# A GRU on one core: the first two steps of x turned by the matrix array, input weights of one gate in four loads, and the state's columns in another order

## The chip, the core and the metric

The kernel runs on one core of one Trainium2 chip. The metric is the device time of one execution in microseconds (us); the value to beat is the median of three runs. One core has five engines with their own instruction queues: TensorE (PE, the matrix array, with its weight loads listed as PEld), VectorE (DVE), ScalarE (ACT), GpSimd (POOL) and SyncE (SP), which issues most of the DMAs. PE writes to PSUM; weights, x and the state lie in SBUF.

## What is computed

A GRU runs over 128 steps on a batch of 64 with 512 inputs and 512 hidden units, and its states are added to its input:

```python
def step(h, inp):
    x_t, prop = inp
    comb = concatenate([x_t, h], axis=-1)
    z = sigmoid(comb @ Wz + bz)
    r = sigmoid(comb @ Wr + br)
    comb2 = concatenate([x_t, r * h], axis=-1)
    h_cand = tanh(comb2 @ Wh + bh)
    h_new = (1.0 - z) * h + z * h_cand
    h_next = where(prop, tanh(h_new @ Wp + bp), h_new)   # prop: every fourth step but the last
    return h_next, h_new
out = x + all h_new
```

All is float32. Each of Wz, Wr and Wh has 512 rows for x (the input weights) and 512 for the state (the state weights).

## The kernel before

The batch is cut into two halves h of 32 rows. A state tile (`h`, `rh`, `c`, `keep`) has 128 partitions, 32 rows of the batch times four quarters q of the columns, and for each half 128 columns. To be multiplied, a state has to be turned: DVE turns blocks of 32 by 32 (`turn`, line 250), which leaves in partition q * 32 + e and block k what was column q * 128 + k * 32 + e. PE then multiplies, for each k of K = 4, a 128 x 32 block of the turned state with rows of the weights that are laid out to fit (`gate`, line 231).

The recurrence, one generator for each half (`half`, line 836), does in every step: PE r's four products; ACT the sigmoid (`crossed`, line 246, two instructions of 64 partitions) into PSUM (`scratch_r`); DVE the product with the state and the turn (`rhT`); PE z's products, ACT its sigmoids into PSUM (`rec_z`); PE the candidate's products on `rhT`, ACT its tanh into SBUF (`c`); DVE a product, a difference and the turn (`hT`), on which the next step's r begins. On every fourth step the state goes through Wp, a tanh (`hprop`) and a turn. The two halves alternate. `seed` (line 395) puts x's share of the gates and the bias into PSUM ahead of the state's products.

The input products of later steps fill the time in which PE would wait for the state. They are put into a list (`put`, `fill`, lines 410 and 416) from which each half takes so many units at the places that a table gives (`PLACES`, `HEAD`, `TAIL`, lines 623 to 630). So the order of PE's work is fixed when the kernel is built. For steps from 4 on they are done with fewer products (sums of weights, prepared by DVE and POOL: `sum_inner`, `sum_outer`; sums of x by POOL: `four`; sums of results: `batch`, `outer_...`).

Before the recurrence stands a prologue. x of steps 0 to 3 is loaded in quarters of the columns (`load_step`, line 110, four DMAs a step) and turned by DVE (`join_x`, line 258). The input weights (`load_wx`, line 116) come r first, in two pieces, then z and the candidate in one piece each, all on SP's queue. `idle(48)` (line 643) gives PE products of zeros meanwhile. Then come r's input products of steps 0 and 1, z's, the bias spread over the partitions by PE (`spread`, line 190), the candidate's, and with `put` and `both(9)` (lines 681 and 682) step 2's. DVE prepares weight sums between and ends with `sum_outer_1` into `d`, on which POOL starts its own sums. The state weights (`load_w`, line 96) are loaded in four pieces of 32 partitions each, on the queues of SP and ACT, at places between the prologue's products; `later_loads` (line 159: x of steps 4 on, Wp, its bias) stand at the prologue's end. POOL issues the loads of the biases (line 130) and of the first state (line 144), and its first full tensor operation is line 659.

POOL adds h to x for the output (line 811), except in the last step, where DVE does (lines 883 and 915).

Of the kernel before, what the change touches and what calls it, by code (L numbers as in the profile page):

```python
# [9 lines left out]
F32 = mybir.dt.float32  # L10
# [8 lines left out]
def kernel(  # L19
# [14 lines left out]
    nc = tc.nc  # L34
    B, T, D = x.shape
    H = h0.shape[1]
    P = 128
# [29 lines left out]
    nc.vector.memset(zeros, 0.0)  # L67
    ones = const.tile([1, V], F32, name="ones")
    nc.gpsimd.memset(ones, 1.0)
# [16 lines left out]
    def part(q):  # L86
        return slice(q * V, (q + 1) * V)

    def load_x(tile_, t0, n, j=0, engs=(nc.sync, nc.sync)):
        for h in range(S):  # L90
            for q in (0, 2, 1, 3):
                engs[q // 2].dma_start(
                    out=tile_[part(q), j : j + n, h, :], in_=x[ts(h, V), t0 : t0 + n, ts(q, J)]
                )

    def load_w(wt, w, k0=0, k1=K, engs=(nc.sync, nc.sync)):
        for q in (0, 2, 1, 3):
            engs[q // 2].dma_start(
                out=wt[part(q), k0:k1, :],
                in_=w[q * P + k0 * V : q * P + k1 * V, :].rearrange("(k e) n -> e k n", e=V),  # L100
            )

    both_queues = (nc.sync, nc.scalar)
# [3 lines left out]
    def new_xr(g):  # L107
        xr[g] = xrp.tile([P, Q4, S, J], F32, tag="xr", name=f"xr_{g}")

    def load_step(t, engs=both_queues):  # L110
        for q in (0, 2, 1, 3):
            engs[q // 2].dma_start(
                out=xr[0][part(q), t], in_=x[:, t, ts(q, J)].rearrange("(h b) u -> b h u", h=S)
            )

    def load_wx(i, k0, k1):
# [2 lines left out]
            in_=gates_in[i][:D].rearrange("(p k) n -> p k n", k=K)[:, k0:k1],  # L119
        )  # L120

    h_init = two.tile([P, S, J], F32, tag="h", name="h_init")
# [12 lines left out]

    for i in (Z, H_):
        load_wx(i, 0, K)

    for t in (2, 3):
        load_step(t, (nc.sync, nc.sync))  # L140
    held = const.tile([1, 1], F32, name="held")
    nc.gpsimd.tensor_copy(held, wx[0:1, 2, R, 0:1])
    for h in range(S):
        nc.gpsimd.dma_start(
            out=h_init[:, h, :],
            in_=h0[ts(h, V), :].rearrange("b (q j) -> q b j", q=NQ),
        )

    def load_wh(i):
        load_w(wh[i], gates_in[i][D:], engs=both_queues)  # L150

    xs = {}

# [34 lines left out]
        return v.rearrange("p n (d c j) -> p c n d j", d=2, c=2)  # L188

    def spread(bank, rows, which):  # L190
        bank = bank.rearrange("p (i d j) -> p i d j", i=2, d=2)
        for h in range(S):
            for c in range(2):
                nc.tensor.matmul(  # L194
                    bank[part(2 * h + c), 0 : len(which)],
                    lhsT=ones,
                    rhs=quarters(bias_row[:, rows])[:, c],
                    start=True,
                    stop=True,
                )  # L200
        for j, i in enumerate(which):
            nc.scalar.copy(
                bias_x[:, :, :, i, :].rearrange("p n d u -> p d n u"),
                bank[:, j].rearrange("p d (n u) -> p d n u", n=C),
            )
# [30 lines left out]
    def product(ps, h, lT, w, k, start=False):  # L236
# [6 lines left out]
            start,  # L243
        )

    def crossed(dst, h, i, func):
        for d in range(2):
            nc.scalar.activation(dst[ts(d, 2 * V)], gate_ps(i, h)[ts(h, 2 * V), d, :], func)  # L248

    def turn(dst, src):  # L250
        nc.vector.transpose(out=dst, in_=src)
# [6 lines left out]
    def join_x(g, i):  # L258
        if g * Q4 >= T:
            return  # L260
        if g not in xT:
            xT[g] = xtp.tile([P, Q4, C, P], F32, tag="xT", name=f"xT_{g}")
        src = xr[g] if g < FIRST else xs[g]
        nc.vector.transpose(
            out=xT[g][:, i].rearrange("p c (a h b) -> p h (c a) b", a=S, h=S),
            in_=src[:, i].rearrange("p h (e k) -> p h k e", k=K),
        )

    def outer(kb, nb, ka):
        return wx[:, kb * S + ka, :, :].rearrange("p g (q n u) -> p n q g u", q=NQ, n=C)[:, nb]  # L270
# [157 lines left out]

    def banks(t):
        first, second = scratch[:2] if t % 2 == 0 else scratch[2:4]  # L430
        rooms = (first[:, : S * J], first[:, S * J :], second[:, : S * J])
        return (rooms[0], rooms[2], rooms[1]) if t == T - 1 else rooms

# [9 lines left out]
    def plain_unit(t, e, k, start, end=None, gates=()):  # L443
        g, i = divmod(t, Q4)
        bank = (q_bank, q_bank, r_bank) if t % 2 == 0 else (a_bank, a_bank, x_banks[0])
        if t == T - 1:
            bank = (a_bank, x_banks[0], a_bank)
        second = H_ if t == T - 1 else Z
# [200 lines left out]
    for i in (1, 2):  # L649
        sum_inner(i, nc.vector, slice(0, 2))  # L650
    spread(scratch[3], slice(0, 2), (R, H_))
    load_wh(R)
    now(first[Z][1])
    for t in range(2):
        add_bias(t, (R,))
    for h in range(S):
        seed(R, 0, h)
    spread(scratch[4], slice(2, 3), (Z,))
    nc.gpsimd.tensor_sub(bias_d, bias_x[:, 1], bias0)
    load_wh(Z)  # L660
    for t in range(2):
        add_bias(t, (Z,))
    seed(Z, 0, 0)
    load_wh(H_)
    join_x(0, 2)
# [5 lines left out]
    now(sum(first[H_], []))  # L671
    for t in range(2):
        add_bias(t, (H_,))
    join_x(0, 3)
# [2 lines left out]
    for i in (3, 5):  # L677
        sum_inner(i, nc.gpsimd)
    sum_outer(3)
    later_loads()  # L680
    put(plain(2, (R, Z)) + plain(3) + plain(2, (H_,)))
    both(9)

# [73 lines left out]
    def behind_step(t, duo, u, h_new):  # L757
# [50 lines left out]
            if u == 7:  # L808
                sum_s12(even + 2)
        if t < T - 1:  # L810
            nc.gpsimd.tensor_add(xr[g][:, j], xr[g][:, j], h_new)  # L811

        n = 0
        if t >= T - CHUNK:
# [21 lines left out]
    def half(h):  # L836

        for t in range(T):
# [31 lines left out]
            def gate_z(part, halves, h_old=h_old, z_=z_, keep=keep):  # L870
                for i in halves:
                    crossed(z_[:, i, :], i, Z, AF.Sigmoid)
                nc.vector.scalar_tensor_tensor(  # L873
                    out=keep[:, part, :],
                    in0=z_[:, part, :],
                    scalar=1.0,
                    in1=h_old[:, part, :],
                    op0=ALU.subtract,
                    op1=ALU.mult,
                )  # L880
                if last:
                    o = xr[g][:, j, part, :]
                    nc.vector.tensor_sub(o, o, keep[:, part, :])

            if h == 1:
                if late(t):
# [25 lines left out]
            nc.vector.tensor_mul(c, cand[:, h, :], c)  # L912
            if last:
                o = xr[g][:, j, h, :]
                nc.vector.tensor_add(o, c, o)
# [87 lines left out]
```

## Time and profile before

| what | us |
|---|---|
| median of three runs (1259.17 to 1260.79) | 1260.61 |
| the profiled execution's own time | 1259.52 |
| its span, first to last instruction | 1257.6 |
| PE busy | 1250.6 |
| POOL busy | 891.5 |
| ACT busy | 837.9 |
| DVE busy | 805.5 |

In the rows that follow, a time in front is the start in us from the span's start, the number behind it the duration; "x16" is a count of instructions merged into a row; brackets hold the idle time of the engine ahead of it and what ended it. A float32 product counts as two records. A group's row gives its busy time in us and the mean duration of one in ns, then the engine's idle time ahead of the group. In the table by stage, each row gives a stretch, its length, then the busy time and count of PE, PEld, DVE, ACT and POOL, PE's granted clock as a share, the share of DMA engines at work, and GB/s.

### The profile page before, as it was taken

The page shows a single profiled execution, that of the slowest core. Times are in us where ns is not written, and L with a number is a line of the kernel's source. Part 1 is how long each engine was busy: PE and PEld are TensorE (multiplying, and loading weights), DVE is VectorE, ACT ScalarE, POOL GpSimd, SP SyncE. Part 2 cuts the span into 40 slices and gives each one's busy share as a digit, 9 for nine tenths or more (in the row PEclk, how much of TensorE's full clock was granted, in tenths as well). Part 3 has the DMA queues.
Part 4 walks back from the last instruction along what each step waited for, and adds up shares of the span by engine and source line. Part 5 has one row for each costly group of instructions (what it writes and reads, how often), then busy time and mean ns, then how long its engine had stood idle before and what let it go on. Part 6 is the DMA issues. An engine that isn't in the chain of part 4 may idle for free.

```text
span 1257.6 us, 60730 instructions
## 1 busy us (share of the span) xinstructions
PE 1250.6 (99%) x25960; PEld 1162.1 (92%) x25960; DVE 805.5 (64%) x2173; ACT 837.9 (67%) x2685; POOL 891.5 (71%) x1031
## 2 busy tenths in 40 slices
PE   9999999999999999999999999999999999999998
PEld 4899999999999999999999999999999999999975
DVE  4666666666666666666666666666666666666545
ACT  2566666767666666766666667667676666676665
POOL 3988877776876778767788676786777777677530
PEclk9999999999999999999999999999999999999999
DMA  8311112121121110211211111111111111111010
GB/s 240 91 28 45 49 41 53 36 54 39 34 53 48 41 47 26 53 53 37 53 29 43 53 43 47 38 47 41 53 37 49 40 37 53 42 48 37 9 42 23
DMA packets 113232, 60.82 MB, mean 48 GB/s; under 512 B 12836, under 2 KB 109348, under 8 KB 112964
## 3 DMA queue, kind: packets, MB, share of 16 engines
q1 hardware_dynamic: 111268, 55.00, 16.4%
q8 instruction: 205, 3.36, 1.1%
q10 hardware_dynamic: 1440, 1.80, 0.6%
q14 instruction: 63, 0.52, 0.1%
q0 software_dynamic: 256, 0.14, 0.1%
HBM read 40.11 MB, written 16.78 MB: 45 GB/s over the span
## 4 chain that ended last, share of the span: by engine, by line
PE 98%; DMA 1%; issue 1%; DVE 0%; SPq 0%; POOLq 0%; POOL 0%; ACT 0%; ACTq 0%
PE rec L222 44%; PE rec_z L222 16%; PE scratch_r L222 14%; PE scratch_q L222 11%; PE scratch_a L222 5%; PE scratch_x L222 4%; PE scratch_y L222 4%; DMA wx<-in_L_cond_Wr_dram 0%; SPq L821 0%; DMA xr<-in_x_dram 0%; DMA out_dram<-xr 0%; PE scratch_x L194 0%; DVE z L912 0%; POOLq L998 0%; POOL xr L811 0%
## 5 line engine op out<-in xcount | busy, mean ns | idle before, releaser
L222 PE MATMUL rec<-wh,rhT 128*32 128x256 f32 x4096 | 376.3, 379 | 0.0
L222 PE MATMUL rec<-wh,hT 128*32 128x256 f32 x3072 | 282.6, 379 | 0.0
L222 PE MATMUL rec_z<-wh,hT 128*32 128x256 f32 x3072 | 282.5, 379 | 0.0
L222 PEld LDWEIGHTS rec<-wh,rhT 128*32 128x32 f32 x4096 | 249.6, 110 | 21.1 <-ACT rec L398 1.2
L248 ACT ACTIVATE scratch_r<-rec 64x128 f32<-64x128 f32 x512 | 128.2, 250 | 138.3 <-PE rec L222 63.7
L398 ACT COPY rec<-cp 64x256 f32<-64x256 f32 x512 | 190.6, 372 | 19.9 <-DVE cp L437 0.4
L222 PEld LDWEIGHTS rec<-wh,hT 128*32 128x32 f32 x3072 | 187.4, 110 | 14.7 <-issue 1.8
L222 PEld LDWEIGHTS rec_z<-wh,hT 128*32 128x32 f32 x3072 | 193.8, 110 | 7.2
L248 ACT ACTIVATE rec_z<-rec_z 64x128 f32<-64x128 f32 x488 | 122.2, 250 | 90.1 <-PE rec_z L222 78.6
L248 ACT ACTIVATE c<-rec 64x128 f32<-64x128 f32 x512 | 139.7, 273 | 60.4 <-PE rec L222 48.8
L811 POOL TENSOR_TENSOR xr<-xr,h 128x256 f32<-128x256 f32 x127 | 93.2, 734 | 91.6 <-DVE h L925 91.6
L575 POOL TENSOR_TENSOR mb<-mb,mb 128x768 f32<-128x768 f32 x58 | 106.3, 1833 | 66.8 <-DVE mb L541 66.8
L575 POOL TENSOR_TENSOR cp<-mb,mb 128x768 f32<-128x768 f32 x76 | 139.2, 1831 | 9.5 <-DVE mb L541 5.8
L575 POOL TENSOR_TENSOR cp<-mb 128x768 f32<-128x768 f32 x46 | 84.2, 1831 | 57.0 <-ACT rec_z L398 55.5
L222 PE MATMUL scratch_r<-tw,s 128*32 128x192 f32 x928 | 120.9, 326 | 0.0
L514 ACT COPY cq<-scratch_q 128x384 f32<-128x384 f32 x212 | 102.1, 482 | 19.3 <-PE scratch_q L222 17.8
L531 DVE TENSOR_TENSOR cx<-scratch_r,cx 128x384 f32<-128x384 f32 x106 | 59.1, 558 | 84.1 <-PE scratch_r L222 66.8
L222 PE MATMUL scratch_q<-tt,s 128*32 128x192 f32 x928 | 103.7, 326 | 0.0
L873 DVE SCALAR_TENSOR_TENSOR keep<-rec_z,h 128x256 f32<-128x256 f32 x91 | 38.7, 425 | 95.6 <-ACT rec_z L248 94.6
L537 DVE TENSOR_TENSOR mb<-scratch_q,cx 128x384 f32<-128x384 f32 x106 | 59.1, 558 | 62.4 <-ACT cq L514 62.4
L853 DVE TENSOR_TENSOR rh<-scratch_r,h 128x128 f32<-128x128 f32 x192 | 56.1, 292 | 61.2 <-ACT scratch_r L248 61.2
L222 PE MATMUL rec<-wp,hT 128*32 128x256 f32 x992 | 91.5, 379 | 0.1
(188 smaller groups left out, 3846.5 us busy)
## 6 DMA issues: line engine op xcount, KB each, us to landing
out_dram<-xr SPq DMA_DIRECT2D x249, 64.0 KB, 1.8
xr<-in_x_dram SPq DMA_DIRECT2D x248, 64.0 KB, 2.1
xs<-in_x_dram SPq DMA_DIRECT2D x240, 64.0 KB, 2.0
wx<-in_L_cond_Wr_dram SPq DMA_DIRECT2D x2, 512.0 KB, 5.1
wx<-in_L_cond_Wz_dram SPq DMA_DIRECT2D x1, 1024.0 KB, 5.9
wx<-in_L_cond_Wh_dram SPq DMA_DIRECT2D x1, 1024.0 KB, 8.2
wp<-in_L_cond_Wp_dram SPq DMA_DIRECT2D x4, 256.0 KB, 5.3
wh<-in_L_cond_Wr_dram ACTq DMA_DIRECT2D x2, 256.0 KB, 3.8
```

The costliest lines, as they stand in the source:

```text
L222: nc.tensor.matmul(ps[part(2 * h + c)], lhsT=left, rhs=rhs(c), start=start, stop=True, skip_group_check=True,)
L248: nc.scalar.activation(dst[ts(d, 2 * V)], gate_ps(i, h)[ts(h, 2 * V), d, :], func)
L398: nc.scalar.copy(gate_ps(i, h)[rows].rearrange("p d (c n) -> p d c n", c=C), G[t][rows, :, :, i, :].rearrange("p c d n -> p d c n"),)
L514: nc.scalar.copy(c[:, :nm], ps[:, :nm])
L531: nc.vector.tensor_add(T2[what][:, :nm], r_ps[:, :nm], T2[what][:, :nm])
L537: nc.vector.tensor_add(blocks(1, 1), runs(q_ps[:, :nm]), runs(T2[what][:, :nm]))
L575: nc.gpsimd.tensor_add(dst, a, b)
L811: nc.gpsimd.tensor_add(xr[g][:, j], xr[g][:, j], h_new)
L853: nc.vector.tensor_mul(rh[:, h, :], r_, h_old[:, h, :])
L873: nc.vector.scalar_tensor_tensor(out=keep[:, part, :], in0=z_[:, part, :], scalar=1.0, in1=h_old[:, part, :], op0=ALU.subtract, op1=ALU.mult,)
```

## The change

x of steps 0 and 1 is loaded as plain rows (64 batch rows, all 512 columns), one DMA on SP and one on ACT; PE turns it with an identity (`turn_rows`: four transposes a step into PSUM) and DVE copies the result. The identity is made on POOL. x of these steps is loaded again later in the old form, for the output. r's input weights come in four loads, one for each k, and r's products of steps 0 and 1 alternate k by k; z's and the candidate's come in two loads each. The idle products are 24, 8 and 4, around the turns.

State weights are loaded in two pieces over 128 partitions, partition p holding rows 4p to 4p + 3. For that the state's columns have to lie in another order: `crossed` writes its result with `state_order`, 32 groups of four elements with a step of 32 elements, and ACT copies the first state in that order. x and the output keep the plain order, so POOL's sum and the last step's operations on DVE read the state with the step. All loads but one are issued on SP, the later ones in one run behind r's input products.

The diff, cut:

```diff
+    ident = const.tile([B, B], F32, name="ident")
+    make_identity(nc, ident)
...
-    def load_w(wt, w, k0=0, k1=K, engs=(nc.sync, nc.sync)):
-        for q in (0, 2, 1, 3):
-            engs[q // 2].dma_start(
-                out=wt[part(q), k0:k1, :],
-                in_=w[q * P + k0 * V : q * P + k1 * V, :].rearrange("(k e) n -> e k n", e=V),
+    def load_w(wt, w):
+        for k0 in (0, 2):
+            nc.sync.dma_start(
+                out=wt[:, k0 : k0 + 2, :],
+                in_=w.rearrange("(p k) n -> p k n", k=K)[:, k0 : k0 + 2],
             )
...
-    load_step(0)
-    load_wx(R, 0, 2)
-    load_step(1, (nc.scalar, nc.scalar))
+    for t in range(2):
+        both_queues[t].dma_start(out=x_rows[:, ts(t, D)], in_=x[:, t, :])
+    for k in range(K):
+        load_wx(R, k, k + 1)
     for i, b in enumerate((br, bh, bz)):
         nc.gpsimd.dma_start(out=bias_row[:, i, :], in_=b.rearrange("(o n) -> o n", o=1))
-    load_wx(R, 2, K)
...
-    for i in (Z, H_):
-        load_wx(i, 0, K)
-    for t in (2, 3):
-        load_step(t, (nc.sync, nc.sync))
+    for k in (0, 2):
+        load_wx(Z, k, k + 2)
+    load_step(2)
+    for k in (0, 2):
+        load_wx(H_, k, k + 2)
...
+    def plain_order(v):
+        return v.rearrange("p (e k) -> p e k", k=K)
+    def state_order(v):
+        return v.rearrange("p (k e) -> p e k", k=K)
     def crossed(dst, h, i, func):
         for d in range(2):
-            nc.scalar.activation(dst[ts(d, 2 * V)], gate_ps(i, h)[ts(h, 2 * V), d, :], func)
+            nc.scalar.activation(
+                state_order(dst[ts(d, 2 * V)]),
+                plain_order(gate_ps(i, h)[ts(h, 2 * V), d, :]),
+                func,
+            )
...
+    def turn_rows(t, bank):
+        for k in range(K):
+            nc.tensor.transpose(
+                bank[:, ts(k, B)],
+                x_rows[:, ts(t, D)].rearrange("b (p k) -> b k p", k=K)[:, k],
+                ident,
+            )
+        nc.vector.tensor_copy(xT[0][:, t].rearrange("p c n -> p (c n)"), bank[:, : K * B])
...
-    idle(48)
-    join_x(0, 0)
-    now(first[R][0])
-    join_x(0, 1)
-    now(first[R][1])
-    now(first[Z][0])
+    idle(24)
+    turn_rows(0, scratch[4])
+    idle(8)
+    turn_rows(1, scratch[3])
+    idle(4)
+    for k in range(K):
+        for t in range(2):
+            now([first[R][t][k]])
+    spread(scratch[4], slice(0, 2), (R, H_))
     load_wh(R)
+    load_step(3)
+    load_wh(Z)
+    load_wh(H_)
+    load_x(xr[0], 0, 2)
+    later_loads()
+    for half_k in (slice(0, 2), slice(2, K)):
+        for t in range(2):
+            now(first[Z][t][half_k])
...
     for h in range(S):
+        nc.scalar.copy(state_order(h_init[:, h, :]), plain_order(h_rows[:, h, :]))
         turn(hT[:, h, :], h_init[:, h, :])
...
-            nc.gpsimd.tensor_add(xr[g][:, j], xr[g][:, j], h_new)
+            o = xr[g][:, j].rearrange("p h (e k) -> p h e k", k=K)
+            nc.gpsimd.tensor_add(o, o, h_new.rearrange("p h (k e) -> p h e k", k=K))
```

More of the change, by code (lines that the diff above doesn't have):

```diff
@@ L144 @@
         nc.gpsimd.dma_start(
-            out=h_init[:, h, :],
+            out=h_rows[:, h, :],
             in_=h0[ts(h, V), :].rearrange("b (q j) -> q b j", q=NQ),
@@ L149, in load_wh @@
     def load_wh(i):
-        load_w(wh[i], gates_in[i][D:], engs=both_queues)
+        load_w(wh[i], gates_in[i][D:])
     xs = {}
@@ L190, in spread @@
     def spread(bank, rows, which):
-        bank = bank.rearrange("p (i d j) -> p i d j", i=2, d=2)
+        bank = bank.rearrange("p (i d j) -> p i d j", i=len(which), d=2)
         for h in range(S):
@@ L267, in join_x @@
         )
+    def turn_rows(t, bank):
+        if 0 not in xT:
+            xT[0] = xtp.tile([P, Q4, C, P], F32, tag="xT", name="xT_0")
+        for k in range(K):
[3 more added lines that the diff above has]
+                ident,
+            )
+        nc.vector.tensor_copy(xT[0][:, t].rearrange("p c n -> p (c n)"), bank[:, : K * B])
     def outer(kb, nb, ka):
@@ L430, in banks @@
         first, second = scratch[:2] if t % 2 == 0 else scratch[2:4]
+        if t < 2:
+            return first[:, : S * J], second[:, : S * J], scratch[4][:, ts(t, S * J)]
         rooms = (first[:, : S * J], first[:, S * J :], second[:, : S * J])
@@ L447, in plain_unit @@
             bank = (a_bank, x_banks[0], a_bank)
-        second = H_ if t == T - 1 else Z
+        second = H_ if t in (1, T - 1) else None if t == 0 else Z
         return (
@@ L670 @@
         sum_inner(i, nc.vector, slice(2, 3))
-    now(sum(first[H_], []))
+    for half_k in (slice(0, 2), slice(2, K)):
+        for t in range(2):
+            now(first[H_][t][half_k])
     for t in range(2):
@@ L881, in gate_z @@
                 if last:
-                    o = xr[g][:, j, part, :]
-                    nc.vector.tensor_sub(o, o, keep[:, part, :])
+                    o = plain_order(xr[g][:, j, part, :])
+                    nc.vector.tensor_sub(o, o, state_order(keep[:, part, :]))
             if h == 1:
```

28 lines of the change are left out of this document (13 added, 15 removed).

## The prediction

> **What bounds the kernel now.** I read the head of the page, then the table by stage, then the chain that ended last.
>
> ```profile
> span 1257.6 us, 60730 instructions
> PE 1250.6 (99%) x25960; PEld 1162.1 (92%) x25960; DVE 805.5 (64%) x2173; ACT 837.9 (67%) x2685; POOL 891.5 (71%) x1031
> PE 98%; DMA 1%; issue 1%; DVE 0%; SPq 0%; POOLq 0%; POOL 0%; ACT 0%; ACTq 0%
> ```
> ```profile
> 11.12:23.74 12.62, 12.62 (x219) 6.58 (x212) 10.28 (x28) 2.14 (x6) 1.11 (x2) 1.00 0.97 236
> 23.74:60.00 36.26, 36.26 (x751) 28.25 (x750) 20.66 (x55) 18.50 (x59) 35.09 (x36) 1.00 0.48 123
> 60.00:1200.00 1140.00, 1140.00 (x23978) 1086.24 (x23971) 743.89 (x1994) 779.46 (x2496) 840.22 (x974) 1.00 0.16 43
> 1253.00:1257.60 4.60, 0.00 (x0) 0.00 (x0) 0.79 (x3) 0.19 (x1) 0.00 (x0) 0.76 0.11 29
> ```
>
> PE is the bound: from 11.12 to 1200 us it is never idle, its granted clock (the 1.00) is full, and the chain lies on it for 98%. So there are two ways to move the end: the moment at which PE has the first gates behind it, and holes torn into a stream that has none. The chain at the start gives the first:
>
> ```profile
> 0.76 1.70 DMA xr<-in_x_dram
> 2.47 5.59 DMA wx<-in_L_cond_Wr_dram
> 8.06 0.04 issue
> 8.11 1.07 PE scratch_q L222 x16
> 9.19 1.93 PE scratch_a L222 x32
> 11.12 1.73 PE scratch_q L222 x32
> ...
> 23.31 0.43 PE scratch_a L222 x8
> 23.74 1.75 PE rec L222 x28
> ```
>
> PE waits for r's input weights until 8.06, has r of steps 0 and 1 done at 11.12, then works 12.6 us without a gap on z, the candidate and step 2, and enters the recurrence at 23.74.
>
> **The change part by part: the start.** Three things must now be there before r's first product: x as rows, the four slices of r's weights, and the identity. The data come early enough: by the chain the first of x landed at 2.47 us, behind an issue at 0.76.
>
> ```profile
> 6.50:8.00 1.50, 1.03 (x16) 0.43 (x16) 0.00 (x0) 0.00 (x0) 0.00 (x0) 1.00 1.07 370
> ```
>
> At 370 GB/s, 0.25 MB of rows and 1 MB of r take 3.5 us from about 2.5, so they are in by 6 to 7. All that follows on SP in one queue (z, step 2, candidate, step 3, nine state and input pieces, together 6.8 MB up to the last state weight) takes 18 us by the same rate, hence is in at about 21; the recurrence needs it from 27 on. The eight loads of x for steps 0 and 1 and step 4's x follow that and are late for nothing. The new queue costs nothing unless the rate falls below 6.8 MB in 24 us, 280 GB/s.
>
> The identity is another matter. It is made on POOL by a memset and a select. In the order of the kernel before, POOL has one instruction that loads engine code, right in front of its first full tensor operation (L659); in the changed order that load stands in front of the select, second thing on POOL.
>
> ```profile
> 0.75 0.12 POOL L69 MEMSET ones<- 1x32 f32 x1 [0.29 <-POOLq L989]
> ...
> 8.23 1.40 POOL L144 DMA_DIRECT2D h_init<-in_cond_dram  x2
> 16.79 1.01 POOL L659 TENSOR_TENSOR bias_d<-bias_x 128x384 f32<-128x384 f32 x1 [7.15 <-ACT bias_x L202]
> ```
>
> Before, the load sits in a gap of 7.15 us in which POOL waited for bias_x in any case, so it costs between 0 and 7.15. The gap is the only row that holds it; I take most of it, 6.5. [...]
>
> So: memset of ones and identity to 1.0, load to 7.5, select 0.3 (as the 0.12 memset and a little), identity at 7.8, seen by PE at 7.9. PE meanwhile runs out:
>
> ```profile
> 1.20 1.04 PE L212 MATMUL rec<-zeros 128*32 128x512 bf16 x8 [1.20 <-DVE zeros L67]
> 2.03 0.64 PE L212 MATMUL rec_z<-zeros 128*32 128x512 bf16 x4
> 2.46 1.07 PE L212 MATMUL rec<-zeros 128*32 128x512 bf16 x8
> ```
>
> Twelve idle products per 1.26 us are 0.105 each: 24 end at 3.8. PE then stands for 4 us. From 7.9: eight turns in two groups, 0.4 a group (two records at 54 ns each, from 1.73 us for 32 of four times the columns, and the first result's latency), 0.8; twelve idle products 1.3, which hide DVE's two copies out of PSUM (0.42 each, as L873 below). r begins at 10.0. Its work is 2 x 1.73 = 3.5. The last row of the stage table shows the clock at 0.76 in 4.6 us without matmuls, so the hole may also cost clock: between 0 and 3.5 (half speed for all of r); I take 1.4, half speed until about 5 us after the restart. r ends at 14.9 instead of 11.12: **+3.8**. That the four slices are used as they come is worth nothing then: all have landed by 10.0.
>
> Behind r PE has the same 12.6 us. DVE, in order too, starts on r's bias at 14.9 + 1.0 (the bias products) + 0.4 (ScalarE's copy) = 16.3; from there to the turn of step 3's x it has no more than the 10.28 us that it had in the stage from 11.12, so this ends by 26.6. PE wants it at 14.9 + 23.31 - 11.12 = 27.1. No further loss; POOL's weight sums, which follow DVE, start as much later as PE does. The biases of r and the candidate are issued on POOL behind the select; the last of the three took longest before:
>
> ```profile
> tw<-in_L_cond_bz_dram POOLq DMA_DIRECT2D x1, 2.0 KB, 5.4
> ```
>
> From 8 to 9.5 plus 5.4 they are in by 13.4 to 14.9, and r's end is 14.9: just covered; uncovered they would cost what they are late.
>
> **State's columns in another order.** Every activation of the recurrence now writes 32 groups of 4 with a step of 32 elements (128 bytes). No row of before shows ScalarE doing so. Its rows:
>
> ```profile
> L248 ACT ACTIVATE c<-rec 64x128 f32<-64x128 f32 x32 | 8.7, 273 | 3.6 <-PE rec L222 2.9
> L248 ACT ACTIVATE scratch_r<-rec 64x128 f32<-64x128 f32 x32 | 8.0, 250 | 8.0 <-PE rec L222 3.7 <-DVE mb L540 3.4
> L811 POOL TENSOR_TENSOR xr<-xr,h 128x256 f32<-128x256 f32 x8 | 5.9, 737 | 4.2 <-DVE h L925 4.2
> L251 DVE STREAM_TRANSPOSE hT<-h 128x128 f32<-128x128 f32 x16 | 5.0, 312 | 0.5
> L264 DVE STREAM_TRANSPOSE xT<-xs 128x256 f32<-128x256 f32 x8 | 4.9, 635 | 0.1
> ```
> ```profile
> L873 DVE SCALAR_TENSOR_TENSOR keep<-rec_z,h 128x256 f32<-128x256 f32 x91 | 38.7, 425 | 95.6 <-ACT rec_z L248 94.6
> L853 DVE TENSOR_TENSOR rh<-scratch_r,h 128x128 f32<-128x128 f32 x192 | 56.1, 292 | 61.2 <-ACT scratch_r L248 61.2
> ACT rec_z L398 <- POOL cp L575: 0.4, 1, 0.4
> ```
>
> (The first five are groups of the eight steps from 600 to 677 us; the last is the one wait for POOL's sums that the list of waits has.) The nearest is L264, DVE reading SBUF with a step of 16 bytes. 128 more columns cost DVE 0.13 (292 ns against 425), so a plain turn of 256 would be 312 + 130 = 442; it takes 635, 0.19 more for 256 elements. For 128 elements that is 0.10 an instruction, a pair 0.19 to 0.2. [...] I take 0.10 where the target is SBUF as in that row (the tanh's c and hprop) and 0 where it is PSUM (the sigmoids of r and z), for which there is no row.
>
> What 0.19 on the tanh does depends on the margin in front of PE:
>
> ```profile
> 600.13 0.55 ACT L248 ACTIVATE c<-rec 64x128 f32<-64x128 f32 x2 [0.68 <-PE rec L222]
> ...
> 601.37 0.31 DVE L251 STREAM_TRANSPOSE hT<-h 128x128 f32<-128x128 f32 x1
> 601.80 0.14 PEld L222 LDWEIGHTS rec<-wh,hT 128*32 128x32 f32 x2
> ...
> 629.96 0.31 DVE L251 STREAM_TRANSPOSE hT<-h 128x128 f32<-128x128 f32 x1
> 630.79 0.14 PEld L222 LDWEIGHTS rec<-wh,hT 128*32 128x32 f32 x2
> ```
>
> c's tanh, two DVE operations, the turn, PE's weight load stand in one line. From the turn's end to the load it is 0.12 in the first pair and 0.52 in the second; hardly one of the 574 turns has less than 0.12, so that is the signal's own time and the first pair has no reserve. The eight turns of first halves from 601.37 to 668.59 have 0.00, 0.13, 0.12, 0.40, 0.41, 0.38, 0.05 and 0.46 of reserve. Against 0.19 the missing parts are 0.19, 0.06, 0.07 and 0.14: 0.46 us in 76.9. The order of PE's work is fixed, so a hole is never made good. Over 1140 us that is 6.8; second halves, whose tanh queues behind the first's on ScalarE, half as much again: **+10**.
>
> POOL's sum of x and h now reads h with that step: at most again 0.74, likelier 0.2 to 0.4 of it. Over 127 times that is 25 to 94 us of the 366 that POOL is idle. What hides it is that hardly anything waits for POOL: 0.4 us in the whole run. At the end four DVE operations of 128 columns read with the step: **+0.3**, 0.1 each, three on the way out.
>
> **The rivals.** *Strides free, identity late.* The start's 3.8 and at most 0.3 remain: 1264 to 1265 us. For it: L264 is a read, and no row shows a write that suffers; against it: L264 is all there is on this step. *PSUM pays as well.* Then z's four sigmoids (+0.4) stand in front of the tanh on ScalarE, which has only 3.6 / 32 = 0.11 us of idle time ahead of each c, and the turn of r*h has the same 0.12 in its tightest step. The tanh chain is late by some 0.4, so the eight reserves miss 0.4, 0.27, 0.28, 0, 0, 0.02, 0.35 and 0, with 0.4 for r's chain 1.7 a cycle, 25 us, and a quarter more for second halves: +31, 1296 us. [...] *The other side: not slower.* If the code load takes under 2 us, as it may if what it loads is there already, the identity is in time. Then 3.8 + 0.8 + 1.3 gives r's start at 5.9 and its end at 9.4, 1.7 us earlier; DVE's chain, then behind PE by 9.4 + 1.4 + 10.28 = 21.1 against 9.4 + 12.2 = 21.6, gives back at most 0.5 where its waits add up. With free strides the time is 1259 to 1259.5. It decides below about 3 us of load; above 5 it can't. *The change doesn't do what it says:* only in the first forecast's sense, that slices used as they come are used when all are there.
>
> **How the numbers follow.** The profiled execution took 1259.5 us (span 1257.6 and 1.9 around it), 1.1 under the median 1260.6. Sum: 1259.5 + 3.8 + 10 + 0.3 = 1273.6, with the 1.1 back 1274.7. Chances: this case 0.37 (own range 1269 to 1283); strides free 0.27; PSUM too 0.22; not slower 0.10; more than that, as from a step that costs the whole 0.27, 0.04. The range 1262 to 1298 leaves out the not-slower case and the last. 0.2% (2.5 us) is about what a measurement of this kernel can tell from no change: faster 0.06, same 0.09 (the not-slower case and a start with little clock loss), slower 0.85.
>
> **What would show it.** Right: PE idle from about 3.8 to 7.9 with the turns behind POOL's select, the select starting some 6 us after its memset; r done near 15 us; c's rows near 370 ns with scratch_r and rec_z still at 250; weight loads that wait for DVE in the tight steps, and PE's busy share falling under 99% between 60 and 1200 us. Wrong: a select before 4 us; c at 273; r's and z's rows at 350, which is the third case; a state weight that lands after 27 us.

## The result, and the profile after

The changed kernel takes 1280.1 us in the median of 5 runs (1277.98 to 1280.64), against 1260.61 before; the ratio is 1.0151, with a 95% interval of 1.0136 to 1.0166. The prediction was 1274.7, in a range of 1262 to 1298. The profiled execution took 1280.1 with a span of 1278.3, 20.7 more than the span before.

The head of the page and the share of the chain:

```profile
span 1278.3 us, 60724 instructions
PE 1268.0 (99%) x25956; PEld 1150.0 (90%) x25956; DVE 811.8 (64%) x2173; ACT 922.5 (72%) x2687; POOL 910.4 (71%) x1033
PE 97%; ACT 1%; DVE 0%; issue 0%; DMA 0%; ACTq 0%; DVEq 0%
```

PE is still "busy" for 99%, and the table by stage (stretch, length, busy us of PE, weight loads, DVE, ACT, POOL, clock, DMA) shows no hole in the middle either (in the last row PE is idle for 8.8 us, against 5.2 in the last 73.2 us before, which hold the same work of VectorE):

```profile
12.03:24.65 12.62, 12.62 (x218) 6.76 (x220) 10.43 (x29) 2.71 (x8) 1.15 (x1) 1.00 1.00 340
60.00:1200.00 1140.00, 1140.00 (x23697) 1060.62 (x23691) 742.80 (x1970) 844.67 (x2467) 855.22 (x973) 1.00 0.16 42
1200.00:1278.30 78.30, 69.50 (x1230) 49.81 (x1219) 36.97 (x119) 54.10 (x153) 15.91 (x13) 0.99 0.12 29
```

The busy share misleads here. The ends of matmuls are modelled, so a hole of 0.2 us disappears under the modelled length of the one before it. What does not disappear is the count: 23,697 records in the same 1140 us, where there were 23,978, 1.2% fewer; the busy time of the weight loads fell too, from 1086.2 to 1060.6. The honest measure is how late a given piece of work is. The turn of r*h happens once per step and half in every kernel here; its end, taken from the trace and set against the kernel before, says where the time goes:

| end of first half's turn of r*h at | before, us | after, us | late by | added in this part |
|---|---|---|---|---|
| step 0 | 26.76 | 27.67 | 0.91 | 0.91 |
| step 8 | 117.12 | 119.08 | 1.97 | 1.06 |
| step 117 | 1162.68 | 1177.62 | 14.94 | 12.97 |
| step 127 (the last) | 1249.07 | 1268.40 | 19.33 | 4.39 |
| end of the span | 1257.64 | 1278.33 | 20.68 | 1.35 |

**The start.** POOL's first instructions (start, us, engine, line):

```profile
0.75 0.12 POOL L69 MEMSET ones<- 1x32 f32 x1 [0.29 <-POOLq L1027]
0.81 0.14 POOL masks.py:197 MEMSET ident<- 64x64 f32 x1
1.03 0.23 POOL masks.py:199 TENSOR_SCALAR_AFFINE_SELECT ident<-ident 64x64 f32<-64x64 f32 x1
```

The select stands 0.22 us behind its memset, and the identity is there at 1.26 us. The record that the prediction read as the load of engine code did move in front of the select. In the views of the two lines (duration in ns: least, median, most; first and last start in us), before and after:

```profile
L659 POOLq MODIFY_POOL_CONFIG  x2: 37/37/37, 9.6 to 9.7; - x2
```
```profile
masks.py:199 POOLq MODIFY_POOL_CONFIG  x2: 1/1/1, 0.9 to 0.9; - x2
```

But no 6.5 us go by behind it: the select follows within about 0.1. What PE waited for instead is in the chain:

```profile
0.76 3.34 DMA x_rows<-in_x_dram
4.10 0.14 issue
4.24 0.71 PE scratch_y L288 x4
...
7.14 0.85 PE scratch_q L227 x6
7.99 0.85 PE scratch_a L227 x6
8.85 0.85 PE scratch_q L227 x6
9.70 0.60 PE scratch_a L227 x6
10.30 0.43 PE scratch_q L227 x6
...
24.65 1.75 PE rec L227 x28
```

x as rows lands at 4.10, and the same piece of r's product takes 0.85 us until 9.7 and 0.43 from 10.3 on: PE runs at half rate until about 10 us. The table by stage counts 36 records in 3.5 us and then 48 in 2.5, while its clock reads 1.00 in both:

```profile
6.00:9.50 3.50, 3.50 (x36) 1.73 (x40) 0.43 (x1) 0.00 (x0) 1.52 (x3) 1.00 0.91 306
9.50:12.00 2.50, 2.50 (x48) 1.16 (x42) 0.00 (x0) 0.00 (x0) 0.00 (x0) 1.00 1.06 328
```

r ends at 12.03, against 11.12, and the recurrence starts 0.91 us later.

**The state's order.** ScalarE's rows over the whole run (count, busy us, mean ns of one, idle before):

```profile
L259 ACT ACTIVATE c<-rec 64x128 f32<-64x128 f32 x512 | 206.5, 403 | 48.7 <-PE rec L227 39.9
L259 ACT ACTIVATE scratch_r<-rec 64x128 f32<-64x128 f32 x512 | 128.0, 250 | 121.7 <-DVE mb L568 68.1 <-DVE cx L559 24.2 <-PE rec L227 13.8
L259 ACT ACTIVATE rec_z<-rec_z 64x128 f32<-64x128 f32 x488 | 122.0, 250 | 81.7 <-PE rec_z L227 70.1
L259 ACT ACTIVATE hprop<-rec 64x128 f32<-64x128 f32 x124 | 50.1, 404 | 8.8 <-PE rec L227 7.2
L259 ACT ACTIVATE z<-rec_z 64x128 f32<-64x128 f32 x24 | 9.5, 395 | 2.5 <-PE rec_z L227 2.1
```

Each instruction that writes SBUF went from 273 to about 400 ns, tanh and sigmoid alike (z is a sigmoid into SBUF in the late steps); the sigmoids that write PSUM have the same 250 ns as before. So it is the target, not the function, that has the price. The turn of h and PE's load, at the same two turns that the prediction showed:

```profile
609.04 0.31 DVE L266 STREAM_TRANSPOSE hT<-h 128x128 f32<-128x128 f32 x1
609.47 0.14 PEld L227 LDWEIGHTS rec<-wh,hT 128*32 128x32 f32 x3 [0.21 <-issue]
...
638.22 0.31 DVE L266 STREAM_TRANSPOSE hT<-h 128x128 f32<-128x128 f32 x1
638.84 0.14 PEld L227 LDWEIGHTS rec<-wh,hT 128*32 128x32 f32 x2
```

At the first the distance is still 0.12, the signal's own time, only PE's weight loads now wait for it ("0.21 <-issue"); at the second it fell from 0.52 to 0.31. Of the eight first-half turns of a cycle five now stand at 0.12. In the view of the tile hT this is a sum: how long the weight loads sat idle before one that reads hT (us, times). Before:

```profile
  issue: 2.3, 8
  ACT z L248: 0.5, 1
  ACT rec_z L398: 0.5, 1
  ACT rec L928: 0.2, 1
```

and after:

```profile
  issue: 8.4, 36
  ACT rec_z L424: 7.2, 33
  ACT z L259: 2.0, 3
  ACT rec L966: 1.7, 2
```

3.5 us became 19.3. The names are not the cause (ACT's copy had long been done where a load waits for a turn); the tile is.

### The profile page after: what moved, and what is told of

It is laid out like the page before. It is cut to its first block, busy times and chain, and to the rows that moved or that the text cites. A ratio compares the mean times of both kernels' runs of the same rounds, so it can differ in the third digit from the quotient of the medians.

```text
span 1278.3 us, 60724 instructions
## 1 busy us (share of the span) xinstructions
PE 1268.0 (99%) x25956; PEld 1150.0 (90%) x25956; DVE 811.8 (64%) x2173; ACT 922.5 (72%) x2687; POOL 910.4 (71%) x1033
## 3 DMA queue, kind: packets, MB, share of 16 engines
q1 hardware_dynamic: 111604, 56.90, 16.4%
## 4 chain that ended last, share of the span: by engine, by line
PE 97%; ACT 1%; DVE 0%; issue 0%; DMA 0%; ACTq 0%; DVEq 0%
PE rec L227 44%; PE rec_z L227 17%; PE scratch_r L227 11%; PE scratch_q L227 10%; PE scratch_a L227 5%; PE scratch_y L227 5%; PE scratch_x L227 5%; ACT c L259 1%; ACT z L259 0%; DMA x_rows<-in_x_dram 0%; DVE h L963 0%; DVE hT L266 0%; ACT rec L424 0%; PE rec L217 0%; DVE z L950 0%
## 5 line engine op out<-in xcount | busy, mean ns | idle before, releaser
L227 PE MATMUL rec<-wh,rhT 128*32 128x256 f32 x4096 | 393.5, 379 | 0.0
L227 PE MATMUL rec<-wh,hT 128*32 128x256 f32 x3072 | 300.4, 380 | 1.6 <-DVE hT L266 1.1
L227 PE MATMUL rec_z<-wh,hT 128*32 128x256 f32 x3072 | 299.7, 379 | 0.0
L227 PEld LDWEIGHTS rec<-wh,rhT 128*32 128x32 f32 x4096 | 254.0, 110 | 19.3 <-ACT scratch_r L259 2.0
L259 ACT ACTIVATE c<-rec 64x128 f32<-64x128 f32 x512 | 206.5, 403 | 48.7 <-PE rec L227 39.9
L227 PEld LDWEIGHTS rec_z<-wh,hT 128*32 128x32 f32 x3072 | 199.8, 110 | 7.4
L849 POOL TENSOR_TENSOR xr<-xr,h 128x256 f32<-128x256 f32 x127 | 111.2, 876 | 99.0 <-DVE h L963 99.0
L950 DVE TENSOR_TENSOR rec_z<-c,rec_z 128x128 f32<-128x128 f32 x244 | 72.3, 296 | 63.2 <-ACT c L259 63.0
L227 PE MATMUL rec<-wp,hT 128*32 128x256 f32 x992 | 97.0, 379 | 0.8 <-DVE hT L266 0.5
L227 PE MATMUL rec<-wh,hpT 128*32 128x256 f32 x992 | 94.3, 379 | 0.0
L227 PE MATMUL rec_z<-wh,hpT 128*32 128x256 f32 x992 | 94.3, 379 | 0.0
```

The costliest lines, as they stand in the source:

```text
L227: nc.tensor.matmul(ps[part(2 * h + c)], lhsT=left, rhs=rhs(c), start=start, stop=True, skip_group_check=True,)
L259: nc.scalar.activation(state_order(dst[ts(d, 2 * V)]), plain_order(gate_ps(i, h)[ts(h, 2 * V), d, :]), func,)
L849: nc.gpsimd.tensor_add(o, o, h_new.rearrange("p h (k e) -> p h e k", k=K))
```

## The experiments

The theory, W: the stepped write to SBUF costs 0.13 us per tanh on the path from gate to turn and makes nearly all of the loss; the start costs 0.9. Its rivals: R, ScalarE pays for a step on either side; P, GpSimd's slower add or the new loads are the cause; S, the new start shifts the two halves against each other for good. Four runs tell them apart. In the table, "late by" is again the turn of r*h (or the end) against the profile of the kernel before; the ratio is that of the times, on the same chip.

| kernel | median us | ratio, 95% | late at step 0 | 8 | 117 | 127 | end |
|---|---|---|---|---|---|---|---|
| after | 1280.10 | 1.0151 (1.0136 to 1.0166) | 0.91 | 1.97 | 14.94 | 19.33 | 20.68 |
| e1_read_side | 1261.12 | 1.0007 (0.9999 to 1.0016) | 1.40 | 1.86 | 1.67 | 1.40 | 2.11 |
| e2_order_off | 1260.76 | 1.0007 (0.9998 to 1.0016) | -0.76 | 0.00 | -0.19 | -0.47 | 0.23 |
| e3_order_alone | 1279.29 | 1.0154 (1.0138 to 1.0169) | 0.45 | 1.48 | 14.49 | 19.03 | 19.88 |
| e4_tanh_only | 1277.21 | 1.0138 (1.0124 to 1.0152) | -0.87 | 1.82 | 14.63 | 16.97 | 17.84 |
| e5_idle32 | 1260.55 | 1.0006 (0.9997 to 1.0015) | 0.59 | 1.99 | 1.85 | 1.60 | 2.36 |
| e6_add_plain | 1260.97 | 1.0007 (0.9999 to 1.0016) | 0.19 | 0.90 | 0.77 | 0.51 | 1.21 |
| e7_first_half | 1267.01 | 1.0058 (1.0043 to 1.0073) | 0.61 | 1.17 | 5.36 | 6.72 | 7.54 |
| e8_steps | 1282.76 | one run, no interval | 0.92 | 1.95 | 17.15 | 21.87 | 23.24 |
| e9_mended | 1261.27 | 1.0002 (0.9994 to 1.0011) | -0.96 | -0.42 | -0.60 | -0.87 | -0.27 |
| e10_gap | 1262.04 | 1.0007 (0.9998 to 1.0016) | 1.26 | 2.94 | 2.83 | 2.76 | 2.84 |
| e11_second_half | 1265.79 | 1.0047 (1.0033 to 1.0061) | -0.21 | 2.25 | 5.80 | 6.71 | 7.42 |
| e12_x_ahead | 1261.20 | 1.0003 (0.9994 to 1.0012) | 0.41 | 1.55 | 1.39 | 1.14 | 1.79 |

**e1_read_side: the step on the other side.** In the changed kernel's activation:

```diff
-                state_order(dst[ts(d, 2 * V)]),
-                plain_order(gate_ps(i, h)[ts(h, 2 * V), d, :]),
+                dst[ts(d, 2 * V)].rearrange("p (k e) -> p k e", k=K),
+                gate_ps(i, h)[ts(h, 2 * V), d, :].rearrange("p (e k) -> p k e", k=K),
```

> The changed kernel, with the reordering of the state's columns put on the other side of ScalarE's instruction: the PSUM bank is read in steps of 16 bytes (p (e k) as p k e) and the SBUF row is written in one piece. The output is the same. Theory W (the write to SBUF with a step of 128 bytes is what costs: 0.13 us per tanh, 19 to 20 of the 20.7 us; the start costs the other 0.9): c's tanh is back near 273 ns at 512 elements on 128 rows in pairs (140 ns each in the mix of forms), and the time is 1260.6 + 0.9 = 1261.5 us, 1260.8 to 1262.5. Rival R (a step costs ScalarE the same on whichever side it stands, now also for the sigmoids, which read PSUM as well): tanh stays near 400 ns, scratch_r and rec_z rise from 250 to about 380, and the time is 1290 or more. Rival P (the loss comes from elsewhere in the change: GpSimd's slower xr add of 876 ns, or the 128-row loads): tanh is short again and the time stays near 1278 to 1280.

**e2_order_off: no reordering in the gates**, both sides of that instruction in one piece.

> The changed kernel with ScalarE's reordering left out of the gates (both sides in one piece); the state's rows then don't match the state weights, so the result is another one, while every other instruction, load and wait stays. Theory W: 1260.6 + 0.9 of the start, 1261.5 us (1260.8 to 1262.5), the margin of the turns ahead of the array as before the change. Rival P (GpSimd's add or the loads): 1275 to 1280, since those are all still there. Rival R makes the same forecast here as W; this run gives the floor against which the run that reads in steps is held: a difference between the two is what the stepped read costs.

**e3_order_alone: the kernel before** with the 128-row state weights, the stepped writes, GpSimd's add and the tail of the change, on its old start.

> The kernel before, start and all, with the new state order alone: state weights on 128 rows, ScalarE's stepped writes, GpSimd's add and the tail reordered. Theory W: 1260.6 + 19.6 = 1280 us (1279 to 1281.5), that is, nearly all of the change's loss without its new start, and the start's 0.9 missing. Rival S (the new start shifts the two chains against each other and that phase lives on in the steady stage): clearly under 1279, the smaller the more of the loss belongs to the phase.

**e4_tanh_only: the step on the tanh alone.**

```diff
-                state_order(dst[ts(d, 2 * V)]),
+                state_order(dst[ts(d, 2 * V)]) if func == AF.Tanh else dst[ts(d, 2 * V)],
```

> The changed kernel with the stepped write left on the tanh alone (c and hprop, in SBUF); the sigmoids (r and z, in PSUM, and z in SBUF in the late steps) write in one piece, so the result is another one. Theory W: PSUM writes take no more with the step (250 ns with and without), so the time stays at 1279 to 1280.5; only the late steps, whose z lies in SBUF, can give back some tenths. If the sigmoids' steps cost something that their rows don't show, the time falls by more than 2 us.

W holds. With the order left out the loss is gone (1.0007), though the loads, the add and the start are all there, so P falls; with the order alone on the old start it is there in full (1.0154), so S falls. And with the step on the reading side the result is the same and the loss is gone too, so R falls. ScalarE's row in e1_read_side:

```profile
L259 ACT ACTIVATE c<-rec 64x128 f32<-64x128 f32 x512 | 138.9, 271 | 61.0 <-PE rec L227 49.3
L259 ACT ACTIVATE scratch_r<-rec 64x128 f32<-64x128 f32 x512 | 128.0, 250 | 137.7 <-PE rec L227 70.6 <-DVE mb L568 50.5 <-DVE cp L465 1.8
```

271 and 250 ns: reading PSUM in steps of 16 bytes is free. The run without any reordering has the same two numbers.

e4_tanh_only came out lower than W said, by more than 2 us against the changed kernel. The table says where: up to step 117 it loses what the changed kernel loses, and from there to step 127 it adds 2.34 instead of 4.39, and 0.87 instead of 1.35 at the end. In these last steps z lies in SBUF; its row is back at 271 ns (395 with the step). The sigmoids into PSUM are indeed free; z's in the late steps cost 2.5 us in sum.

**e7 and e11: one half's tanh alone.** As e4_tanh_only, with "and h == 0" or "and h == 1" added to the condition.

> The changed kernel with the stepped write left on the tanh of the first half of the batch alone; the other half's and the sigmoids write in one piece, so the result is another one. With the step on both halves' tanh alone the kernel took 16.5 us more than with none. The prediction held that the first halves' turns, whose margins are short, carry two thirds of the loss: 1260.8 + 11 = 1271.8 us (1270.5 to 1273). Rivals: both halves carry the same, 1269; the second halves carry none, 1277.

> The changed kernel with the stepped write left on the tanh of the second half of the batch alone (the result is another one). Steps on the first half's tanh alone cost 6.2 us over the run without any, steps on both 16.4. If the two halves' losses add, the second half alone costs 10.2: 1260.8 + 10.2 = 1271 us. If a late turn of one half is partly covered by the other half's work, and only both late together leave the array without any, it costs about as much as the first alone: 1266 to 1268. By the prediction's share (one third) it would be 1266.3, so the first reading and the prediction are told apart, the second and the prediction are not.

Against the 1260.8 of e2_order_off the first half alone costs 6.2 us, the second alone 5.0, both together 16.4 (the medians are of different chips; the ratios, each to the kernel before on its own chip, give 6.4, 5.0 and 16.5). Two thirds for the first, as predicted, is wrong, and so is a plain sum: 5.2 us come only when both are late. The profiles of e4_tanh_only and e11_second_half also lose 1.8 and 2.0 us at step 0, where x landed late (VectorE waited 2.8 and 3.0 us for it), and that is not the step's. The middle is free of it: per cycle of eight steps (steps 16 to 112 hold twelve) the loss is 0.30, 0.26 and 0.92.

With the first half alone the weight loads did wait: the sum of idle time before loads of hT is 13.5 us, 10 more than in the kernel before, but its turn of r*h fell behind by only 5.55 us between step 8 and step 127. The reading that fits is that a late turn of one half is partly covered by the other half's products; how the cover works step by step was not traced.

**e8_steps: other steps.** The same instruction with 32 runs of 4 for c (16 bytes apart), 8 runs of 16 for hprop (64 bytes), 2 of 64 for z (256 bytes).

> Other steps of the write to SBUF, each on an instruction of its own (the result is another one): c with 16 bytes between neighbours (32 runs of 4), hprop with 64 bytes (8 runs of 16), z of the late steps with 256 bytes (2 runs of 64). If every element written apart from its neighbour costs the same, all three take near 400 ns and the time stays near 1278 to 1280. If the price comes with the step's size, 16 bytes is cheaper than 128: c under 330 ns and the time well under 1270. If runs set it, z is the cheapest.

```profile
L270 ACT ACTIVATE c<-rec 64x128 f32<-64x128 f32 x512 | 212.3, 415 | 47.6 <-PE rec L227 38.9
L270 ACT ACTIVATE hprop<-rec 64x128 f32<-64x128 f32 x124 | 48.8, 393 | 8.4 <-PE rec L227 6.4
L270 ACT ACTIVATE z<-rec_z 64x128 f32<-64x128 f32 x24 | 9.6, 399 | 2.5 <-PE rec_z L227 2.1
```

393 to 415 ns for steps of 16 to 256 bytes: in these rows the price is one for elements apart, nearly whatever the distance, about 1 ns for each of the 128 (122 to 144 ns over the 271 of one piece). It also hints at a slope: 12 ns more on c's tanh (and 11 less on hprop's) made the span 2.6 us longer than the changed kernel's, 1280.9 against 1278.3. It is a single run, and the changed kernel's own spans lie 2.7 us apart; the middle is firmer, with 1.10 us lost per cycle against 0.92 to 0.94 in the three profiles with 403 ns.

**e5_idle32: no gap ahead of the turns**, on top of e1_read_side.

```diff
-    idle(24)
+    idle(32)
```

> The kernel that reads PSUM in steps, with 32 warm-up products instead of 24 ahead of the first turns, so that the array is fed until x_rows lands. Theory G (a gap of 0.28 us or more at about 4 us makes the array start again on its 5 us at half rate; gaps of 0.19 and 0.21 us did not): products of r at full rate from the first one, 0.43 us a group of 8, r done near 10.3 us in the profile, first turn of r*h near 26.0 us (before 26.76). Where the profiled run of the reading kernel had 28.16. From step 7 on the lead of 0.77 us is gone again, as it was in the run without the order, since the array then waits for GpSimd's sums; with 0.7 us more at the tail the time is 1260.3 us, 1259.5 to 1261. Rival (half rate for another reason, such as the f32 turns themselves): half rate again until about 10 us, first turn of r*h at 27.5 to 28.2.

The half rate is gone. PE's first stretches:

```profile
4.64 0.69 PE L288 MATMUL scratch_y<-ident,x_rows 64*128 64x64 f32 x4
5.26 0.61 PE L217 MATMUL rec<-zeros 128*32 128x512 bf16 x8
...
6.65 0.60 PE L227 MATMUL scratch_q<-wx,xT 128*32 128x256 f32 x8
7.08 0.60 PE L227 MATMUL scratch_a<-wx,xT 128*32 128x256 f32 x8
...
10.21 0.64 PE L227 MATMUL scratch_q<-wx,xT 128*32 128x256 f32 x8 [0.80 <-DMA wx<-in_L_cond_Wr_dram]
```

A group of 8 starts every 0.43 us from 6.65 on, and with the same spacing in the three other kernels without the gap (e6, e9, e12). But theory G's limit of 0.28 us falls: e11_second_half has a gap of 0.40 and runs r's products at full rate from the first one as well. And the time of the kernel did not move: PE, now fast, meets r's last slices, which landed at 10.2 in this run, and the recurrence starts 0.59 us later than before. In e2_order_off and e9_mended the same slices came in time, and the start was 0.76 and 0.96 us early. What the new start is worth hangs on when x_rows and these slices land, and that moves from one run to the next: the first turn, where PE waited for x_rows, began between 4.14 us (e2_order_off) and 4.55 (e1_read_side), and the first product with the last slice at 9.12 without a wait in e9_mended, at 10.21 behind a wait of 0.80 here.

**e10_gap: a gap made on purpose.** In the kernel before:

```diff
-    idle(48)
+    idle(26)
```

> The kernel before with 26 warm-up products instead of 48, so that the array stands idle from about 4.0 us until its first products of r at about 6.5 us; nothing else is changed. Theory G (after such a gap the array takes 5 us at half rate again): groups of 16 products take 1.7 instead of 0.87 us until about 11.5 us, less what the wait of 0.57 us for wx hides, so the first turn of r*h comes 1.5 us later than 26.76 and the time is 1261.5 us (1260.8 to 1262.3). Rival (the rate rises some 6 us after the start whatever the array does): full rate from 6.5 us on, and no change.

```profile
6.99 3.42 PE L222 MATMUL scratch_q<-wx,xT 128*32 128x256 f32 x32 [2.62 <-DMA wx<-in_L_cond_Wr_dram]
10.22 1.92 PE L222 MATMUL scratch_a<-wx,xT 128*32 128x256 f32 x32
```

32 records take 3.4 us after the gap and 1.9 from 10.2 on, so the rival (full rate at a fixed time) falls. The start is 1.26 us late, near the 1.5 expected, and 1.68 more are lost at step 0, where in this run a state weight and then x came late. In the time, +1.5 us in the medians, the interval still holds no change.

**e6_add_plain: GpSimd's add without the step**, on top of e5_idle32.

> The same with GpSimd's add of h to xr in one piece on both sides (so the columns that are added are the wrong ones). Theory Q (GpSimd's add, 876 ns with the step against 734 without, is 1.0 us late in sum by step 7, and that is what the array waits for at scratch_x behind scratch_a near 99.6 us): the add is 734 ns again, the hole near 99.6 us is gone, and the lead of 0.77 us over the kernel before lives on to the end: 1259.5 us, 1258.7 to 1260.2. Rival (a transfer or another sum sets that point): hole and time as in the run beside it, 1260.3.

The add is back at 734 ns, and the loss near step 7 is still there (0.19 late at step 0, 0.90 at step 8). This theory fell. What starts late is GpSimd's whole chain of sums. Before, and in e6_add_plain:

```profile
23.64 0.18 POOL L676 COPY held<-d 1x1 f32<-1x1 f32 x1 [5.84 <-DVE d L310]
```
```profile
25.01 0.17 POOL L714 COPY held<-d 1x1 f32<-1x1 f32 x1 [7.12 <-DVE d L336]
```

VectorE's new order at the start hands over d 1.4 us later; from there GpSimd goes through the same work with the same longest pause (2.51 us near 70) to the sums s4r, which begin at 100.30 instead of 99.30, and PE waits for them.

**e9_mended and e12_x_ahead: the new start mended.** On top of e5_idle32, s4r goes ahead of its neighbours at step 5, and z and c of the last step stay in the plain order; e12 also loads xr[1] ahead of xr[0].

> The kernel with 32 warm-up products and stepped reads, with two more edits: at step 5 GpSimd makes the sums s4r ahead of the three sums of 768 columns that stood before them, and in the last step z and c are left in the plain order, so that the tail's two instructions on VectorE and its stores see rows in one piece. Theory (the loss of 0.7 to 1.0 us near 99.6 us is the array waiting for s4r, which GpSimd reaches late because it starts its chain of sums at 25.0 to 25.4 us instead of 23.6, and the 0.7 us after the last r*h is the tail's stepped access): from step 4 to step 8 no lead is lost, the last 7.3 us are those of the kernel before, and the time is 0.7 + 0.7 us under the run with 32 warm-up products, 1259.2 us (1258.4 to 1260). Rival for the first (the sums behind become late in turn): the loss comes back at a step after 7. Rival for the second (the order of the last loads and stores): the tail keeps its 0.7 us.

> The mended kernel (stepped reads, 32 warm-up products, s4r ahead at step 5, plain last step), with the loads of x for steps 4 to 7 issued ahead of those of steps 0 and 1 (which only GpSimd's add reads, from 45 us on). Theory: in the mended kernel's profile the transposes of x at step 0 waited 1.59 us for x to land at 32.4 us, and what stood behind them on VectorE lost 0.6 us; eight transfers of some 0.4 us to issue stand ahead, so x lands about 3 us earlier and that wait goes: the early start of 0.8 to 1.0 us is kept, and the time is 0.4 us under the mended kernel's and 0.3 to 0.7 us under the kernel before on the same chip, if r's weights land as early as in that profile. Rival: the transfers are bound by their bandwidth or land late for other reasons, or r's weights land late: as the mended kernel, ratio 1.000.

In e9_mended the loss near step 7 is gone (0.41 early at step 6, 0.44 at step 7), so the first theory holds in this run. The tail's is not: VectorE's last operations take 3.5 us from the last turn as before, but 4.4 us pass from the last of them to the end of the span, against 3.8. The same stretch is 4.15 to 4.45 in every kernel with the new start and 3.7 to 3.9 in the three with the old, so it belongs to the new start's transfers or to how they are counted at the end; it was not isolated. In e9_mended a wait on VectorE ate a part of the early start:

```profile
32.46 1.24 DVE L281 STREAM_TRANSPOSE xT<-xr 128x256 f32<-128x256 f32 x2 [1.59 <-DMA xr<-in_x_dram]
```

That wait is gone in e12_x_ahead. But there r's slices landed late again (a wait of 0.95 us), and 0.42 and 0.75 us are lost on the way to step 8. The second of them, from step 7 to 8, is what the rival of e9's first theory said: the weight loads wait 0.88 us, until 111.8, for the next of GpSimd's sums, s. The time is that of the kernel before, ratio 1.0003. No version found here beats it.

## Why the prediction was right and wrong

**Right: the direction, the mechanism of most of it, and where it costs nothing.** The tanh's rows rose and those of scratch_r and rec_z stayed at 250, as the first case had it; weight loads wait for DVE in the tight steps; GpSimd's add (876 ns for 734, +0.14, under the 0.2 to 0.4 estimated) is hidden: e6_add_plain shows no gain without it. No state weight was late in the profile after.

**Wrong by size: the order's +10, which is some 18** (12.97 + 4.39 in the first table, and most of the 1.06 ahead of step 8: 0.72 of it is lost by step 4, where e1_read_side and e2_order_off, without any stepped write, lose nothing; e4 and e2 put the tanh's part alone at 16.4). Four parts of that step failed. The price was taken from a read by DVE, 0.10 for an instruction; it is 0.13. "A hole is never made good" is wrong for one half alone: with the measured 0.26 for a pair the prediction's own reserves miss 0.74 us a cycle in first halves, and e7_first_half lost 0.30. The second halves were given half of the first's loss; alone each costs about the same, and both together more than the sum. These errors pull in different directions: with the right price the same rule would have given 1.11 a cycle, and 0.94 was measured. And the rate of the middle was laid over 1140 us, as if the end were like the middle: the ten last steps lose 4.39 us in 86, four times the middle's rate. There z's sigmoids write SBUF as well, which e4 puts at 2.05 of it; that less filling work stands there between a turn and its use is likely the rest, but was not tried alone. The predicted sign that PE's share would fall under 99% between 60 and 1200 us did not come; it could not, since the modelled ends cover holes of this size.

**Wrong in its mechanism: the start's +3.8, which is 0.9.** "That load stands in front of the select" came true; the step that failed is its price, 6.5, which is about 0.1. The gap of 7.15 us from which it was read holds the load's record (37 ns, at 9.6) and a wait for bias_x; that the load took most of the gap was the author's estimate, and "a select before 4 us" was the sign against it: 0.22 us lie between the memset and the select, which starts at 1.03. Two things in that part were right for another reason: PE does run out (24 products end at 3.96, and x_rows lands at 4.10, where the prediction reckoned with 2.47 for the first of x), and it pays in rate: r's eight groups take 4.94 us from 6.92 on where eight of 0.43 would take 3.46, so 1.5 against the 1.4 that the author estimated for half speed until 5 us after the restart (here some 5.7, from 4.24 to about 9.9). The case "not slower" was right about the start as such: in the runs in which x and r's slices came in time the recurrence began 0.8 to 1.0 us early (1.7 was forecast). It kept back 0.5 us for DVE's chain; what was lost behind it went to GpSimd's late sums instead, 0.4 to 1.0 at step 7 in e1, e2, e5 and e6.

**Wrong: the tail's +0.3**, which is 1.35 from the last turn of a first half. 0.98 of it lie between that turn and the end of VectorE's last operation. VectorE's own steps are 0.20 of that (so much is left in e5_idle32, where ScalarE's instructions are short), near the estimate; the rest came with the longer z and c in front of them. The other 0.37 lie behind, in the new start's longer end, which the prediction did not look at.

In the spans the sum was 6.6 us short, since two errors partly cancelled: 2.9 too much at the start, 9.5 too little behind it. That the forecast came as near as it did is in part luck.

## What to carry to other kernels

If an order has to change on the way through ScalarE, put the step where PSUM is, on the read: the result is the same, and here it made 19 us of difference (271 ns a tanh against 403). Price a longer instruction by the reserve of each turn in front of the engine that binds, in the last steps separately, but try how much of such a wait stays: with one half late less than half of it did. Judge holes of 0.2 us by counts or by how late a marked piece of work is, never by the busy share. A start that gains a microsecond must be followed to the next thing that is late (here r's slices, x for step 4, then GpSimd's sums); none of them shows before the first is gone.

## What the runs showed of the hardware

- ScalarE, 64 x 128 float32 out of PSUM: 271 to 273 ns into SBUF in one piece (before, e1_read_side, e2_order_off), 393 to 415 with neighbours 16 to 256 bytes apart (after, e8_steps); into PSUM 250 without a step (before) and with one of 128 bytes (after). With PSUM read in steps of 16 bytes the rows are 271 and 250 (e1_read_side), the same as without any step (e2_order_off).
- PE's rate early in the run: seven profiles have 24 warm-up products and then a gap. With gaps of 0.28, 0.32, 0.46 and 0.59 us (after, e7_first_half, e8_steps, e1_read_side) full rate came only at 9.3 to 10.6 us; with 0.19, 0.21 and 0.40 (e2_order_off, e4_tanh_only, e11_second_half) by 5 to 6. So the length of the gap does not decide alone, and what else does was not shown. Fed without a gap, PE reached full rate between about 4 us (e12_x_ahead) and 6 us (before). From the end of a gap that cost the rate to full rate it took 3.2 us (e10_gap) to 6 us (e1_read_side). The granted clock read 1.00 at half rate and at full rate alike (3 to 12 us in the profile after, 5 to 10 in e1_read_side), so it is the spacing of the products that tells.
